# Normalising the next image on two engines: the even channel chunks of every image move from ScalarE to VectorE

## The chip, the cores and the metric

The kernel runs on one core of a Trainium2 chip. A core has a matrix engine (TensorE, PE in the profile; its weight loads are shown as PEld), a vector engine (VectorE, DVE), an activation engine (ScalarE, ACT), a general engine (GpSimd, POOL) and a synchronising engine (SyncE, SP). Each engine executes its own list of instructions strictly in that list's order, and semaphores order the lists against each other. POOL, SP and ACT also issue transfers (DMAs). The metric is the device time of one execution in microseconds (us), as a median of several executions.

## The reference

For each of 16 images of 512 channels by 1024 positions (float32): group normalisation over 8 groups of channels, a projection to query, key and value, attention in 4 heads of 128 channels, an output projection, and the image itself added at the end.

```python
xg = x.reshape(b, 8, -1)
xn = ((xg - mean(xg)) * rsqrt(var(xg) + 1e-5)).reshape(b, c, h, w)
xn = xn * norm_gamma + norm_beta
qkv = einsum('oc,bchw->bohw', qkv_w, xn) + qkv_b
q, k, v = split(qkv, 3)                       # 4 heads of 128 each
attn = softmax(q @ k.T * 128 ** -0.5)         # 1024 x 1024 per head
out = attn @ v
out = einsum('oc,bchw->bohw', proj_w, out) + proj_b
return x + out
```

## The kernel before

The kernel walks through 512 steps: 16 images, 4 heads each, 8 blocks of 128 keys per head. A step computes the scores of one block against all 1024 queries (two matmuls of 512 columns, L764), their exponential on ScalarE (L770), and, one step later, the weighted sum with the values (L860). VectorE adds the exponentials up (`tot`, L776 and L778). Between these, `plan_head` puts the other work of neighbouring images into the steps of a head:

- in head 1 of image b: the output projection of image b-1 (`proj_groups`, tiles `pp_...`), the loading of image b+1, its statistics, and then its normalisation (`normalise`, in steps 5 and 6, two channel chunks of 128 in each, each chunk in two halves of 512 columns);
- in head 2: queries and keys of the first two heads of image b+1 (`qk_groups`); in head 3: its values (`v_groups`).

The projections are done by Strassen's scheme at two levels. At the outer level, sums of the blocks of x are formed (`sums_of_b`, L280: `x` in place, then `xt`). At the inner level there are four groups of products. In a group, `make_sum` (L533) builds sums t1 to t4 on VectorE, and PE multiplies seven products in the order p1, p2, p6, p5, p7, p4, p3 (`strassen`). p1 and p2 take unsummed blocks, p6 takes t2, p5 takes t1, p7 t3, p4 t4. Products land in two accumulators `x` and `y`; ScalarE copies some out (L458, L581), and VectorE combines them into `r` (L583). The accumulator tag `y` has two buffers, so p5 of a group cannot begin before VectorE has combined p2 of the same group.

The output projection ends in `finish` of `proj_groups`: VectorE writes a tile `y` (L743), POOL issues a transfer that adds the image to it in place (L747, `accum_op`), waits until that has landed, and issues the transfer to `out` (L748). The tiles come from `ypool`, tag "y", with four buffers; eight such tiles are written per image, so the writing of a later one waits until the transfer to `out` of the tile four before it has landed.

Statistics are reduced on ScalarE (L243 to L249), combined by `stats_group` on PE, VectorE and POOL (L50 to L78), and give a scale `sc` and a shift `sh` per channel. `Norm.apply` then works in place on a half chunk, either as an activation on ScalarE (L85) or as a two-operation instruction on VectorE (L88). In image 0, whose normalisation stands before everything else, odd chunks go to ScalarE and even ones to VectorE; for every later image all chunks go to ScalarE.

The program is not issued in source order: a planner simulates the work with its own cost estimates and lays out one list of instructions for each engine. `tc.high_priority` moves the copies out of the accumulators, the combinations and the exponentials forward. So a change in one operation's engine can move others in every list.

Of the kernel before, what the change touches and what calls it, by code (L numbers as in the profile page):

```python
# [162 lines left out]
def fast_path(ctx, tc, x, sources, out, consts, flag, dims):  # L163
# [68 lines left out]
    norm = Norm(nc, gn, ps_a, avg, neghalf, gamma_sb, beta_sb, NCC, N, "y")  # L232
# [22 lines left out]
    def normalise(b, c, half):  # L255
        t = xs[b, c][:, ts(half, HALF)]
        sc, sh = scaled[b]

        return norm.apply(t, t, sc, sh, c, b > 0 or c % 2 == 1)


    def halves(tiles, prefix):
# [494 lines left out]
    def where(s):  # L757
        bh, j = divmod(s, NB)
        return (*divmod(bh, HEADS), j)
# [242 lines left out]
    def plan_head(b, h):  # L1002
# [9 lines left out]
        elif h == 1:  # L1012
            if b > 0:
                spread(plan, staggered(proj_groups(b - 1)), 0, NB)
            if b + 1 == B:
                plan[0].append(lambda: last_loads("x"))
            else:
                plan[0].append(lambda: load_x(b + 1))
                spread(plan, [lambda c=c: stats_chunk(b + 1, c) for c in range(NCC)], 2, 4)
                plan[4].append(lambda: stats_group(b + 1))  # L1020
                for r in range(2):
                    plan[5 + r] += [
                        lambda c=c, half=half: normalise(b + 1, c, half)
                        for c in range(KC * r, KC * r + KC) for half in range(NH2)
                    ]
                plan[6].append(lambda: x_sums(b + 1, (1,)))
# [41 lines left out]
    for half in range(NH2):  # L1068
        for c in range(NCC):
            ins = normalise(0, c, half)  # L1070
            last_normal = ins if c % 2 == 0 else last_normal
# [15 lines left out]
    for s in range(steps + 1):  # L1087
        units = []
        if s < steps:
            b, h, j = where(s)  # L1090
# [159 lines left out]
```

## Time and profile before

| | |
|---|---|
| median of 3 runs | 3227.11 us (3226.0 to 3231.77) |
| the profiled execution | 3226.0 us, of which its span 3224.1 us |
| PE busy | 3161.0 us (98% of the span) |
| VectorE busy | 2563.3 us (80%) |
| ScalarE busy | 1440.8 us (45%) |
| GpSimd busy | 565.7 us (18%) |
| normalisation on ScalarE (L85) | 124 instructions, 814 ns each |
| normalisation on VectorE (L88, image 0 only) | 4 instructions, 542 ns each |
| mean granted TensorE clock | 0.999 |

A line of a timeline gives the start, the time from the start of the first to the end of the last instruction of the row, the engine, the source line, the operation, output and inputs by the program's names, the shapes and the number of instructions; in square brackets the idle time of the engine just before and what ended it. Instructions on one engine overlap a little, so that two starts can be closer together than the duration of one. A table by windows gives, for each stretch of time, its length, the busy time of the five engines with the number of instructions, the granted TensorE clock, the busy share of the DMA engines and what they moved.

### The profile page before, as it was taken

The page shows a single profiled execution, that of the slowest core. Times are in us where ns is not written, and L with a number is a line of the kernel's source. Part 1 is how long each engine was busy: PE and PEld are TensorE (multiplying, and loading weights), DVE is VectorE, ACT ScalarE, POOL GpSimd, SP SyncE. Part 2 cuts the span into 40 slices and gives each one's busy share as a digit, 9 for nine tenths or more (in the row PEclk, how much of TensorE's full clock was granted, in tenths as well). Part 3 has the DMA queues.
Part 4 walks back from the last instruction along what each step waited for, and adds up shares of the span by engine and source line. Part 5 has one row for each costly group of instructions (what it writes and reads, how often), then busy time and mean ns, then how long its engine had stood idle before and what let it go on. Part 6 is the DMA issues. An engine that isn't in the chain of part 4 may idle for free.

```text
span 3224.1 us, 33936 instructions
## 1 busy us (share of the span) xinstructions
PE 3161.0 (98%) x10474; PEld 2185.4 (68%) x10474; DVE 2563.3 (80%) x4505; ACT 1440.8 (45%) x2709; POOL 565.7 (18%) x922
## 2 busy tenths in 40 slices
PE   8999999999999999999999999999999999999999
PEld 6566676676667766676666666667666676666764
DVE  8878878787887878777787777987878877788774
ACT  2535435354353543534435454453534445344332
POOL 0011212112121121211212111121111211112110
PEclk9999999999999999999999999999999999999999
DMA  5654655546555465554655546465464654646541
GB/s 168 220 180 131 201 157 153 180 131 206 157 171 166 129 198 160 175 165 128 201 159 168 168 125 205 156 179 165 125 195 154 186 177 124 188 147 193 166 128 49
DMA packets 217067, 526.92 MB, mean 163 GB/s; under 512 B 32816, under 2 KB 65840, under 8 KB 216880
## 3 DMA queue, kind: packets, MB, share of 16 engines
q1 hardware_dynamic: 128992, 276.88, 28.0%
q0 software_dynamic: 73920, 212.39, 22.2%
q10 hardware_dynamic: 13968, 35.41, 3.4%
q8 instruction: 86, 1.41, 0.2%
q14 instruction: 101, 0.83, 0.1%
HBM read 389.56 MB, written 135.00 MB: 163 GB/s over the span
## 4 chain that ended last, share of the span: by engine, by line
PE 66%; issue 19%; DVE 6%; DMA 6%; POOL 2%; ACT 0%; SPq 0%; POOLq 0%; ACTq 0%; DVEq 0%
PE s L764 18%; PE po L860 18%; PE qk_x L563 10%; PE qk_y L563 7%; PE v_x L563 6%; PE v_y L563 4%; DMA y<-in_x 3%; DVE qk_t L533 2%; DMA out_y<-y 2%; DVE xt L280 1%; DVE qk_r L583 1%; POOL y L747 1%; DVE part L789 1%; POOL rstd L67 0%; DVE tt L787 0%
## 5 line engine op out<-in xcount | busy, mean ns | idle before, releaser
L764 PE MATMUL s<-qk,qk 128*128 128x512 f32 x2048 | 1048.2, 593 | 3.2 <-ACT p L770 3.2
L860 PE MATMUL po<-p,v 128*128 128x512 f32 x2048 | 1049.4, 594 | 0.0
L770 ACT ACTIVATE p<-s 128x512 f32<-128x512 f32 x1024 | 610.4, 597 | 943.5 <-PE s L764 934.5
L860 PEld LDWEIGHTS po<-p,v 128*128 128x128 f32 x2048 | 605.0, 302 | 326.8 <-issue 219.6
L778 DVE TENSOR_TENSOR tot<-tot,p 128x1024 f32<-128x1024 f32 x385 | 469.8, 1220 | 175.4 <-ACT p L770 173.7
L764 PEld LDWEIGHTS s<-qk,qk 128*128 128x128 f32 x2048 | 387.7, 190 | 96.9 <-issue 31.4
L563 PEld LDWEIGHTS qk_x<-qk_t,w 128*128 128x128 f32 x1344 | 251.7, 190 | 168.1 <-issue 76.3
L563 PE MATMUL qk_x<-qk_t,w 128*128 128x256 f32 x1344 | 356.4, 382 | 1.4 <-ACT qk_u L458 1.4
L458 ACT COPY qk_u<-qk_x 128x512 f32<-128x512 f32 (+1 forms) x256 | 136.3, 533 | 231.6 <-PE qk_x L563 226.2
L720 POOL DMA_DIRECT2D vd<-vu x120 | 66.9, 559 | 918.7 <-DVE vu L712 916.7
L747 POOL DMA_DIRECT2D y<-in_x x120 | 109.4, 1038 | 537.2 <-DVE y L743 525.0
L563 PE MATMUL pp_x<-pp_t,w_proj 128*128 128x256 f32 x630 | 169.3, 385 | 20.8 <-ACT pp_p L458 20.8
L583 DVE TENSOR_TENSOR qk_r<-qk_y,qk_u 128x512 f32<-128x512 f32 (+1 forms) x256 | 157.4, 615 | 36.9 <-ACT qk_u L458 22.8
L563 PEld LDWEIGHTS pp_x<-pp_t,w_proj 128*128 128x128 f32 x630 | 116.0, 190 | 90.1 <-ACT pp_p L458 29.6
L725 POOL DMA_DIRECT2D v<-vd x240 | 140.7, 593 | 190.6 <-DMA vd<-vu 87.2
L563 PE MATMUL v_x<-v_t,w_v 128*128 128x256 f32 x630 | 166.6, 381 | 0.0
L583 DVE TENSOR_TENSOR v_r<-v_y,v_u 128x512 f32<-128x512 f32 (+1 forms) x120 | 76.3, 636 | 110.6 <-ACT v_u L458 80.3
L537 POOL DMA_DIRECT2D kept_t<-qk_t x240 | 143.4, 600 | 107.9 <-DVE qk_t L533 92.5
L563 PEld LDWEIGHTS v_x<-v_t,w_v 128*128 128x128 f32 x630 | 118.4, 190 | 55.3 <-issue 19.1
L563 PE MATMUL qk_y<-x,w 128*128 128x256 f32 x512 | 141.7, 379 | 0.0
L655 DVE SCALAR_TENSOR_TENSOR qk<-qk_r,qkb_sb,qk_r 128x512 f32<-128x512 f32 x192 | 137.7, 744 | 1.6
L563 PE MATMUL qk_y<-qk_t,w 128*128 128x256 f32 x448 | 119.1, 382 | 19.5 <-DVE qk_r L583 19.5
(204 smaller groups left out, 4353.5 us busy)
## 6 DMA issues: line engine op xcount, KB each, us to landing
kept_t<-qk_t POOLq DMA_DIRECT2D x180, 256.0 KB, 5.5
w<-kept SPq DMA_DIRECT2D x90, 512.0 KB, 4.3
v_t<-kept_t SPq DMA_DIRECT2D x180, 256.0 KB, 2.9
w<-kept SPq DMA_DIRECT2D x90, 384.0 KB, 3.6
rinv<-row ACTq DMA_DIRECT2D x63, 512.0 KB, 5.1
x<-in_x POOLq DMA_DIRECT2D x60, 512.0 KB, 4.9
vd<-vu POOLq DMA_DIRECT2D x120, 256.0 KB, 3.0
v<-vd POOLq DMA_DIRECT2D x240, 128.0 KB, 4.1
```

The source lines that it names most:

```text
L458: nc.scalar.copy(t[n][:, :width], t["x"][:, :width])
L537: nc.gpsimd.dma_start(t, to)
L563: nc.tensor.matmul(acc[:, ts(i, Q)], have["w"][t][:, i, slot, :], inner(i, bn), start=(first and i == 0), stop=True, skip_group_check=True,)
L583: nc.vector.tensor_add(dst, view(a), view(c))
L655: nc.vector.scalar_tensor_tensor(st[b, h][:, ts(half, HALF)], a, qkb_sb[:, i : i + 1], c, ALU.add, ALU.add)
L720: nc.gpsimd.dma_start(rows[which][ts(h, P), :], u)
L725: nc.gpsimd.dma_start(vs[b, pair][ts(q, BLK), half].rearrange("m h (k i) j -> m (h k) (i j)", k=n), rows[which].rearrange("(k m) (q e) -> ...
L747: nc.gpsimd.dma_start(t, x[b, ts(o, P), ts(half, HALF)], accum_op=ALU.add)
L764: nc.tensor.matmul(sc, ks[b, h][:, ts(j, P)], qs[b, h][:, ts(half, HALF)], start=True, stop=True)
L770: exps[s] = nc.scalar.activation(ps[s][:, ts(half, HALF)], sc, AF.Exp, scale=SCALE)
L778: added[b, h, j] = nc.vector.tensor_add(tot[b, h][:, i], tot[b, h][:, i], ps[s][:, i])
L860: nc.tensor.matmul(po[b, h][:, i], v_block(b, h, j), ps[s][:, i], start=(j == 0), stop=(j == NB - 1),)
```

## The change

In `normalise`, the condition that sends a half chunk to ScalarE loses its first alternative. For images 1 to 15, chunks 1 and 3 stay on ScalarE and chunks 0 and 2 go to VectorE, as in image 0.

```diff
     def normalise(b, c, half):
         t = xs[b, c][:, ts(half, HALF)]
         sc, sh = scaled[b]
-
-        return norm.apply(t, t, sc, sh, c, b > 0 or c % 2 == 1)
+        return norm.apply(t, t, sc, sh, c, c % 2 == 1)
```

`Norm.apply` (L81 to L88) is as before:

```python
        if on_scalar:
            return self.nc.scalar.activation(
                xn, x, AF.Identity, bias=sh[:, i], scale=sc[:, i]
            )
        return self.nc.vector.tensor_scalar(xn, x, sc[:, i], sh[:, i], ALU.mult, ALU.add)
```

The lines after it have numbers lower by one in the changed kernel.

## The prediction

> **What bounds the kernel now.** I read the page's busy table first, then the table by windows of 40 us, then PE's own timeline for its gaps, and last, around one image's gaps, the timelines of VectorE, POOL and ScalarE. PE is the bound:
>
> ```profile
> PE 3161.0 (98%) x10474; PEld 2185.4 (68%) x10474; DVE 2563.3 (80%) x4505; ACT 1440.8 (45%) x2709; POOL 565.7 (18%) x922
> ```
>
> Work that moves off ScalarE (45%) is worth nothing by itself. What counts is where PE is idle, and in windows that is one place per image, the end of head 1, where the moved instructions are. Around the normalisation of image 8:
>
> ```profile
> 1480.00:1520.00 40.00, 40.00 (x135) 28.21 (x134) 31.07 (x62) 25.43 (x58) 1.41 (x3) 1.00 0.34 106
> 1520.00:1560.00 40.00, 36.99 (x123) 25.12 (x122) 34.26 (x71) 19.61 (x35) 16.64 (x25) 1.00 0.79 198
> 1560.00:1600.00 40.00, 39.61 (x132) 27.87 (x133) 31.16 (x50) 15.06 (x28) 4.49 (x9) 1.00 0.62 208
> ```
>
> The first busy figure is PE: 40.00, 36.99, 39.61. PE's timeline has two gaps there:
>
> ```profile
> 1532.52 0.70 PE L563 MATMUL pp_x<-pp_t,w_proj 128*128 128x256 f32 x2 [1.62 <-ACT pp_p L458]
> ...
> 1544.68 1.03 PE L563 MATMUL qk_x<-qk_t,w 128*128 128x256 f32 x4
> ...
> 1560.39 1.13 PE L563 MATMUL qk_y<-qk_t,w 128*128 128x256 f32 x4 [1.77 <-DVE qk_r L583]
> ```
>
> Gap 1 (0.95 to 1.63 us in images 2 to 15) waits for a copy on ScalarE that stands behind the first normalisation, which waits for its shift. Gap 2 (0.88 to 1.80 us in images 3 to 15, together 19.6 us) waits until VectorE has combined p2 of the second group. The middle line is p6 of the first group, which needs t2 and begins without a wait. VectorE and POOL in the same stretch:
>
> ```profile
> 1540.41 0.41 DVE L533 TENSOR_TENSOR qk_t<-x,qk_t 128x256 f32<-128x256 f32 x1
> 1544.39 1.42 DVE L743 SCALAR_TENSOR_TENSOR y<-pp_r,projb_sb,pp_r 128x512 f32<-128x512 f32 x2 [3.56 <-DMA out_y<-y]
> 1545.72 0.76 DVE L533 TENSOR_TENSOR qk_t<-qk_t,x 128x256 f32<-128x256 f32 x2
> ```
>
> ```profile
> 1532.67 2.85 POOL L747 DMA_DIRECT2D y<-in_x  x3 [3.12 <-DVE y L743]
> 1539.61 0.58 POOL L748 DMA_DIRECT2D out_y<-y  x1 [4.09 <-DMA y<-in_x]
> ```
>
> VectorE sits 3.56 us at its seventh `y` tile until the transfer of the third has left its buffer: issued at 1532.67 with the added image, sent out at 1539.61, free at 1544.39. PE survives this wait only because t1 and t2 (the last of them at 1540.41) stand ahead of it.
>
> **What the change moves.** Per image, four ScalarE instructions (814 ns, L85) become four VectorE instructions. Their price is in image 0:
>
> ```profile
> 14.97 1.92 DVE L88 TENSOR_SCALAR x<-x,sc,sh 128x512 f32<-128x512 f32 x4
> ```
>
> That is 542 ns each, and one every (1.92 - 0.54) / 3 = 0.46 us. VectorE's page total rises by 60 x 0.54 = 32 us, ScalarE's falls by 60 x 0.81 = 49 us. Neither is on the path as a sum; places decide. The changed kernel's issue lists show: PE's and SP's are the same except in image 1. ScalarE's differ only by the missing four and small swaps; a normalisation (now chunk 1) still stands just ahead of the copy of gap 1 and waits for the same shift, so **gap 1 stays**: 0. On VectorE, the same in images 2 to 15, the planner did more than insert:
>
> ```
> sh; pp_t2; L88 x_0 (both halves); y_2_1, y_3_1; pp_t3; pp_r; y_2_0, y_3_0; pp_t4;
> L88 x_2; tot; pp_r; L88 x_2; x_0, x_1 (L280); pp_r; tot;
> y_0_1, y_1_1;  t1 (2);  qk_r of p2;  t2 (2);  t3 ...
> ```
>
> Before, t1 and t2 stood ahead of `y_0_1`; now they stand behind it, and so behind its wait. No DMA moves but some stores of t1 and t2 behind two L747 on POOL; their readers come some 10 us later: 0.
>
> **The new wait, image 8.** y_2_1 is written two L88 later: 2 x 0.46 = 0.92. POOL's chain from it (6.9 us to the landing, 4.8 to leaving) shifts as a whole, so `y_0_1` starts at 1544.39 + 0.92 = 1545.3. VectorE reaches it at about 1541.3, so the transfer still ends last. `y_1_1` started 0.66 us after it, at 12.53 us after gap 1. Behind the start of `y_1_1`: itself 0.66, t1 0.67, the combination of p2 0.60, the first half of t2 0.42, hand-over 0.1 (gap 2's ended 0.06 us after VectorE): 2.45. So p6 can begin 12.53 + 0.92 + 2.45 = 15.90 us after gap 1; PE is due there at 1544.68 - 1532.52 = 12.16. **New gap 3.74 us**, in-order PE with scores and values queued behind it.
>
> All images: the start of `y_1_1` after gap 1 is 11.64 to 12.57 us in images 3 to 15 (sum 159.45), and PE is due at 12.16 wherever I looked but in image 2. Sum of new gaps 159.45 + 13 x (0.92 + 2.45 - 12.16) = 45.2 us, 2.85 to 3.78 each. In image 2 p6 is due at 13.85, `y_1_1` starts at 11.00: 0.5 us. Together **+45.7**. Lower bound if the landing does not shift (other traffic sets it): 45.7 - 14 x 0.92 = 33. Upper, if VectorE's landing wait grows by POOL's usual spread (L747 lasts 0.86 to 1.55 us): 45.7 + 14 x 0.6 = 54. I take the middle row, image 8's own chain.
>
> **Gap 2 goes.** From the start of `y_1_1` VectorE needs, by the trace's spacings, 14.6 us to the combination gap 2 waits for (which the new list puts ahead of t3 and t4 of its group, 1.3 us earlier); PE, at p6 2.45 us after that start, needs it 13.9 us later, 16.4. With 1.8 us to spare: **-19.6**; bound 0 if a step is late. What is late next is nothing that I find: t3 of that group is ready 3 us ahead of p7.
>
> **Image 1** has no projection. Here two of PE's waits (0.56 and 0.70, for exponentials behind normalisations) go, and two pairs for the values move ahead of a wait of 0.41 for weights: **-1.5**; bounds -1.9 (all four of its waits) and +1.8 (four L88 on the path).
>
> **The clock.** Image 2 shows what idle time can cost beyond itself: there a gap of 0.27 stood just before the 1.62.
>
> ```profile
> 334.00:337.50 3.50, 1.61 (x6) 0.97 (x6) 3.50 (x9) 2.02 (x4) 0.76 (x2) 1.00 0.01 2
> 337.50:341.00 3.50, 3.50 (x6) 1.37 (x5) 3.50 (x6) 2.63 (x5) 1.96 (x3) 0.51 0.75 153
> ```
>
> The granted clock fell to 0.51 for 3.5 us, 1.7 us lost, after 1.89 us idle in 3.5. Gaps of up to 1.80 alone did not cause it. New gaps of about 3.5 us are twice that, so I expect a drop in nearly all of images 3 to 15: upper 13 x 1.7 = 22, lower 0; I take 13 x 1.4 = **+18**, since part of the slow stretch may fall into the gap itself. [...]
>
> [...]
>
> **Sum.** 45.7 - 19.6 - 1.5 + 18 = +42.6 us on the profiled execution's 3226.0 us (span 3224.1 and 1.9 around it): 3268.6. The median of the runs shown is 1.1 above it, so 3269.7; I say 3269, 1.3% slower.
>
> **Rivals.**
> - New gaps without a clock drop: +25, 3251. For it: 26 gaps of 0.9 to 1.8 us kept the clock. Against: these are twice as long.
> - The landing does not shift and the clock holds: 33 - 19.6 - 1.5 = +12, 3239. For it: in image 9 the same wait ended 1.3 us earlier than in image 8, so it is not fixed.
> - Worse: gap 2 stays, or a clock drop lasts twice as long: about +20 more, 3289. For it: VectorE gets 1.83 us more work where it is 86% busy. Against: the 1.8 us to spare, and a slow PE only adds to it.
> - Faster, one mechanism: the wait for the `y` buffer vanishes (POOL's transfer leaves early). Then VectorE runs straight through, `y_1_1` starts at about 9.4 us after gap 1, p6 is not late, gap 2 goes: -21, 3206. The new gap equals gap 2's 1.5 us when `y_1_1` starts 10.3 us after gap 1, before the shift of 0.92; so the leaving transfer would have to land 2 us earlier than on average now (12.27). All 13 images speak against it.
> - That the change does nothing (within 0.2%, 6.5 us, about what a measurement can tell) needs the landing some 1.5 us earlier and a clock that holds: 45.7 - 14 x 1.5 - 21.1 = +4.
>
> **How the numbers follow.** Forecast 0.54, no clock drop 0.22, no shift 0.08, worse 0.07, faster 0.06, no change 0.03. Slower holds the first four, 0.91. The range leaves out faster, no change, and half of the worst: from 3239 to 3292.
>
> **What would show it.** After: a gap of about 3.5 us at `qk_x<-qk_t` (p6) some 12 us behind gap 1 in images 3 to 15, ended by VectorE; VectorE's list with L743 waiting for `out_y` about as long as now and `qk_t` behind it; no gap 2; slices with the clock at 0.5 behind the new gap; gap 1 as before. Wrong if L743 no longer waits, if gap 1 goes too (20.7 us in images 2 to 15), or if the clock holds.

## The result, and the profile after

The changed kernel takes 3269.89 us (median of 5, 3263.51 to 3271.43) against 3229.22 us (median of 5) for the kernel before: ratio 1.0121, 95% interval 1.0106 to 1.0136. It is 1.2% slower; 3269 us was forecast. The profiled execution took 3269.89 us, span 3268.1 us, mean granted TensorE clock 0.992. The page's busy row:

```profile
PE 3183.4 (97%) x10474; PEld 2197.0 (67%) x10474; DVE 2590.0 (79%) x4565; ACT 1404.8 (43%) x2649; POOL 564.4 (17%) x922
```

The span grew by 44.0 us. PE's busy time accounts for 22.4 of it (3161.0 to 3183.4, for the same 10474 matmuls, so these ran slower), and PE's idle time for 21.6 (63.1 to 84.7). The view of PE's waits (us in total, times, longest) says where it is idle; first the kernel before:

```profile
PE pp_x L563 <- ACT pp_p L458: 20.8, 14, 1.6
PE qk_y L563 <- DVE qk_r L583: 19.5, 13, 1.8
```

and the changed kernel:

```profile
PE qk_x L562 <- DVE qk_t L532: 39.9, 14, 3.4
PE pp_x L562 <- ACT pp_p L457: 21.9, 14, 1.6
```

Gap 1 (`pp_x`) stayed, gap 2 (`qk_y`) went, and a wait of p6 (`qk_x`) for VectorE's sums came: 39.9 - 19.5 + 1.1 = 21.5 us, which is all the new idle time. Image 8 on PE's timeline of the changed kernel:

```profile
1550.76 0.70 PE L562 MATMUL pp_x<-pp_t,w_proj 128*128 128x256 f32 x2 [1.62 <-ACT pp_p L457]
...
1566.07 2.04 PE L562 MATMUL qk_x<-qk_t,w 128*128 128x256 f32 x4 [2.99 <-DVE qk_t L532]
...
1581.59 1.03 PE L562 MATMUL qk_y<-qk_t,w 128*128 128x256 f32 x4
```

p6 in the second row waits 2.99 us and then takes 2.04 instead of 1.03 us: the clock is at half. The third row is p5 of the second group, where gap 2 was. VectorE's timeline at the same place shows what p6 waits for:

```profile
1562.78 1.54 DVE L742 SCALAR_TENSOR_TENSOR y<-pp_r,projb_sb,pp_r 128x512 f32<-128x512 f32 x2 [3.22 <-DMA out_y<-y]
1564.23 0.75 DVE L532 TENSOR_TENSOR qk_t<-x 128x256 f32<-128x256 f32 x2
1564.90 0.68 DVE L582 TENSOR_TENSOR qk_r<-qk_y,qk_p 128x512 f32<-128x512 f32 x1
1565.51 0.75 DVE L532 TENSOR_TENSOR qk_t<-x,qk_t 128x256 f32<-128x256 f32 x2
```

t1 (second row) and t2 (last row) stand behind the tile that waits for its buffer, and p6 starts when the first half of t2 is there. POOL's side of that buffer:

```profile
1551.82 2.84 POOL L746 DMA_DIRECT2D y<-in_x  x3 [4.03 <-DVE y L742]
1557.90 0.58 POOL L747 DMA_DIRECT2D out_y<-y  x1 [3.24 <-DMA y<-in_x]
```

From issue to leaving is 6.08 us here; the kernel before had 6.94. The clock, by windows placed behind three gaps of the changed kernel (length, then busy times; the granted clock is the third figure from the end):

```profile
758.00:761.50 3.50, 3.34 (x12) 2.62 (x13) 3.50 (x9) 1.07 (x2) 3.08 (x5) 1.00 0.66 149
...
1146.00:1149.50 3.50, 3.38 (x5) 1.79 (x6) 3.50 (x8) 2.92 (x6) 2.19 (x3) 0.53 0.35 67
...
1566.00:1569.50 3.50, 3.43 (x8) 2.84 (x9) 3.50 (x8) 0.59 (x1) 3.22 (x5) 0.51 0.65 141
```

Behind the new gap of image 8 (last row) it is 0.51 for 3.5 us. Behind that of image 4 (first row, gap 3.06 us) it holds, and behind gap 1 of image 6 (middle row, 1.62 us) it drops. Images 2 to 14 have 12 half-clock stretches, nine of 3.41 us and three of twice that; about 1.7 us are lost in each 3.41: 25.6 us of clock, part of it inside gaps. The kernel before had one such stretch there.

### The profile page after: what moved, and what is told of

Read it like the earlier page. It is cut to its first block, busy times and chain, and to the rows that moved or that the text cites. A ratio compares the mean times of both kernels' runs of the same rounds, so it can differ in the third digit from the quotient of the medians.

```text
span 3268.1 us, 33904 instructions
## 1 busy us (share of the span) xinstructions
PE 3183.4 (97%) x10474; PEld 2197.0 (67%) x10474; DVE 2590.0 (79%) x4565; ACT 1404.8 (43%) x2649; POOL 564.4 (17%) x922
## 4 chain that ended last, share of the span: by engine, by line
PE 71%; issue 20%; DMA 5%; POOL 2%; DVE 2%; ACT 0%; POOLq 0%; SPq 0%; DVEq 0%; ACTq 0%
PE s L763 19%; PE po L859 19%; PE qk_x L562 12%; PE qk_y L562 8%; PE v_x L562 6%; PE v_y L562 4%; DMA y<-in_x 2%; DMA out_y<-y 2%; POOL y L746 1%; DVE y L742 1%; POOL rstd L67 0%; PE v_x L672 0%; PE lx L943 0%; POOL out_y L747 0%; DVE qk_t L532 0%
## 5 line engine op out<-in xcount | busy, mean ns | idle before, releaser
L777 DVE TENSOR_TENSOR tot<-tot,p 128x1024 f32<-128x1024 f32 x385 | 469.7, 1220 | 176.4 <-ACT p L769 173.9
L562 PE MATMUL qk_x<-qk_t,w 128*128 128x256 f32 x1344 | 365.7, 389 | 41.0 <-DVE qk_t L532 39.9
L582 DVE TENSOR_TENSOR qk_r<-qk_y,qk_u 128x512 f32<-128x512 f32 (+1 forms) x256 | 158.3, 618 | 51.2 <-ACT qk_u L457 37.8
L582 DVE TENSOR_TENSOR v_r<-v_y,v_u 128x512 f32<-128x512 f32 (+1 forms) x120 | 76.1, 634 | 110.5 <-ACT v_u L457 80.3
L711 DVE STREAM_TRANSPOSE vu<-vt 128x512 f32<-128x512 f32 x120 | 134.7, 1122 | 1.4 <-DMA vd<-vu 1.4
```

The source lines that it names most:

```text
L562: nc.tensor.matmul(acc[:, ts(i, Q)], have["w"][t][:, i, slot, :], inner(i, bn), start=(first and i == 0), stop=True, skip_group_check=True,)
L582: nc.vector.tensor_add(dst, view(a), view(c))
L711: nc.vector.transpose(u.rearrange("p (q i j) -> p j q i", q=n, i=BLK), t.rearrange("p (j q i) -> p j q i", q=n, i=BLK),)
L777: added[b, h, j] = nc.vector.tensor_add(tot[b, h][:, i], tot[b, h][:, i], ps[s][:, i])
```

## The experiments

The theory: VectorE's work does not matter by its amount, but by what stands behind the wait for the output buffer. The rivals: the four added VectorE instructions are a cost by themselves; or it is the clock. Each ratio is to the kernel before, run beside it on the same chip; its median there was 3232.74 us (E1 to E4), 3222.72 (E5, E6), 3220.71 (E7 to E9) and 3223.69 (E10, E11).

**E1 and E2: take away what the tile waits for.** In the changed kernel (E1) and in the kernel before (E2), the last two output tiles of an image are written into a half of an accumulator that is no longer read, instead of into `ypool`.

```diff
...
-        R = {}
+        R = r_tiles[name] = {}
...
-            t = ypool.tile([P, HALF], F32, tag="y", name=f"y_{b}_{o}_{half}")
+            if which == "c12":
+                t = r_tiles[f"pp_{b}"][2][:, 1, r, :]
+            else:
+                t = ypool.tile([P, HALF], F32, tag="y", name=f"y_{b}_{o}_{half}")
```

> The changed kernel, with the last two output tiles of an image (y_0_1, y_1_1) written into a used-up half of R[2] in place of the ypool, so that VectorE needn't wait for a buffer there. Theory (t1 and t2 stand behind that wait): no wait at the seventh tile, the new gap of 1.2 to 3.4 us at p6 goes, gap 2 stays away, the clock holds behind p6: 3203 to 3212 us, below the kernel before. Rival A (four more instructions on a VectorE 86% busy there cost what they last, wherever they stand): still slower than before, 3240 to 3265 us.

> The kernel before with the same other buffer for the two tiles. Theory: the 3.4 us wait on VectorE goes, and with it gap 2 (19.6 us in all): 3204 to 3212 us, the same as the run with the changed kernel to within 5 us, since then the engine of the normalisation decides nothing. Rival A: 25 to 45 us below the changed kernel with the same buffers. If gap 2 has another cause: 3226 us.

E1 took 3206.76 us, ratio 0.992 (0.9904 to 0.9937); E2 3201.48 us, ratio 0.9906 (0.989 to 0.9923), 2.5 us below its range. PE's waits and VectorE at image 8 in E1:

```profile
PE pp_x L562 <- ACT pp_p L457: 22.1, 14, 1.6
```

```profile
1534.01 1.41 DVE L745 SCALAR_TENSOR_TENSOR pp_r<-pp_r,projb_sb,pp_r 128x512 f32<-128x512 f32 x2
1535.34 0.76 DVE L532 TENSOR_TENSOR qk_t<-x 128x256 f32<-128x256 f32 x2
1536.01 0.68 DVE L582 TENSOR_TENSOR qk_r<-qk_y,qk_p 128x512 f32<-128x512 f32 x1
1536.61 0.75 DVE L532 TENSOR_TENSOR qk_t<-x,qk_t 128x256 f32<-128x256 f32 x2
```

In E2 gap 1 is likewise the one wait of head 1 that is left:

```profile
PE pp_x L563 <- ACT pp_p L458: 21.3, 14, 1.6
```

The order on VectorE in E1 is that of the changed kernel, but the tile no longer waits, and of the two gaps of head 1 only gap 1 is left. PE's busy time fell to 3160.0 us; besides the end one half-clock stretch is left. So the wait for the buffer is the cause of the new gap and with it of the slow clock, and in the kernel before it is the cause of gap 2 as well, since E2 has no gap 2 either. Without that wait the two divisions of the normalisation differ by 5.3 us, 0.16%, a little more than the 5 us that were expected; the runs of the two do not overlap (3203.65 to 3208.05 us against 3200.57 to 3202.94), and the cause of this rest stays open.

**E3 and E4: order alone.** E3 is the changed kernel with t1 and t2 of the first group put ahead of the tile again. E4 is the kernel before, normalisation all on ScalarE, with t1 held behind the eighth tile.

```diff
+            early = sums == "keep" and g == 0 and m in ("t1", "t2")
+            with tc.high_priority(URGENT) if early else ExitStack():
...
```

```diff
...
+            late_sums = sums == "keep" and g == 0 and m == "t1" and (b - 2) in final_y
+            with tc.issue_after(final_y[b - 2].ins) if late_sums else ExitStack():
...
-            nc.vector.scalar_tensor_tensor(
+            final_y[b] = nc.vector.scalar_tensor_tensor(
```

> The changed kernel, with t1 and t2 of the first group of queries and keys given the priority of the copies, so that VectorE does them ahead of the seventh output tile again; wait, buffers and the four moved instructions stay. Theory: the new gap at p6 goes, the clock holds, gap 2 comes back at 1.5 to 2.5 us: 3222 to 3240 us. Rival A: 3255 to 3272 us.

> The kernel before (normalisation all on ScalarE), with t1 of the first group held behind the eighth output tile: the order of the changed kernel without its change of engine. Theory: a gap at p6 of some 2.0 us (12.27 + 0.66 + 0.67 + 0.52 - 12.16), gap 2 goes, the clock drops in about half of the images: 3232 to 3256 us. Rival A: order alone costs nothing, 3222 to 3231 us.

E3 took 3226.95 us, ratio 0.9982 (0.9973 to 0.9992); E4 3243.59 us, ratio 1.0045 (1.003 to 1.0061). The waits of E3, then of E4:

```profile
PE pp_x L566 <- ACT pp_p L457: 22.3, 14, 1.6
PE qk_y L566 <- DVE qk_r L586: 13.1, 13, 1.1
```

```profile
PE qk_x L568 <- DVE qk_t L536: 24.6, 23, 2.3
```

With the sums ahead of the tile the changed kernel has the gaps of the kernel before (gap 2 back, 1.07 us in most images) and, within 0.2%, its time; with the sums behind it the kernel before gets the new gap without one instruction more on VectorE, and the clock dropped in eight of its images, in two of them behind gap 1. So the order costs. The four added instructions led the planner to that order; the loss is larger with them (1.2% against 0.45%). In image 8 the last tile then starts 12.80 us after gap 1 (12.44 in E4), and p6 another 2.51 us later (1.90 in E4, whose list has half of t2 ahead of a combination).

**E5: half of the change.** Only chunk 2 goes to VectorE.

```diff
-        return norm.apply(t, t, sc, sh, c, c % 2 == 1)
+        return norm.apply(t, t, sc, sh, c, (b > 0 and c == 0) or c % 2 == 1)
```

> Half of the change: only chunk 2 goes to VectorE, chunk 0 stays on ScalarE (two instructions per image moved, not four). In its list the first half of t1 stands ahead of the seventh output tile, the second half and t2 behind it. Theory: the third tile isn't delayed, p6 is late by 12.27 + 0.66 + 0.34 + 0.52 - 12.16 = 1.6 us per image, too short for the clock, and gap 2 goes: 3220 to 3236 us, no half of the loss. Rival A (work): half of it, 3240 to 3252 us.

3222.05 us, ratio 0.9998 (0.9988 to 1.0007).

```profile
PE qk_x L562 <- DVE qk_t L532: 17.9, 12, 2.4
```

Half the change is not half the loss. The new gap is 17.9 us in all and replaces gap 2 at about its price, and the clock fell twice at this place (images 4 and 11, gaps of 2.28 and 2.42 us). In image 8 the planner put half of t1 ahead of the waiting tile, so PE waits for less behind it.

**E6: the clock by itself.** The changed kernel with ten idle matmuls of 128 columns ahead of p6 in images 2 to 15, so that PE is not idle for as long.

```diff
+    fill = {f"qk_{b}_0_0": 10 for b in range(2, B)}
...
+            if name in fill:
+                t["y"] = bank("y")
+                for _ in range(fill[name]):
+                    nc.tensor.matmul(t["y"][:, :P], avg, ones_sq, start=True, stop=True, ...)
             mm(t["x"], 6, False)
...
```

> The changed kernel, with ten idle matmuls of 128 columns (about 2.1 us) ahead of p6 of the first group in images 2 to 15, into the accumulator that p5 overwrites: work that nobody needs, inside the new gap. Theory (the clock's drop behind the gap is a cost of its own, some 22 us in all): the granted clock holds behind p6 and the time falls to 3242 to 3256 us although PE has more to do. Rival B (the gap alone costs, the clock's drop is hidden): 3266 to 3274 us, or more.

3250.62 us, ratio 1.0085 (1.0068 to 1.0102), span 3251.6. The idle matmuls by line, and the waits:

```profile
L474 PE MATMUL qk_y<-ones_sq,avg 128*128 128x128 f32 x280 | 33.5, 275 | 0.0
```

```profile
PE pp_x L571 <- ACT pp_p L458: 14.3, 14, 1.6
PE qk_x L571 <- DVE qk_t L541: 14.0, 14, 2.1
...
PE qk_y L571 <- DVE qk_r L591: 6.3, 13, 0.5
```

The clock dropped once. PE's busy time is 3194.6 us; without the 33.5 of the idle matmuls 3161.1, the 3161.0 of the kernel before. So the 22.4 us of extra busy time in the changed kernel are the clock. The span fell by less, 16.5 us: the idle matmuls and the rest of the wait are together 47.5 us in place of 39.9, gap 1 is 7.6 less, and 6.3 us of gap 2 came back. That last wait belongs to this run's own list, in which sums for later products stand ahead of the combination it waits for: this starts 13.8 us after p6 in image 8, against 11.4 us in image 4 of the changed kernel, where the clock held as well.

**E7, E8 and E9: can gap 1 go too?** All normalisations of an image are put into step 6, and those on ScalarE are held behind the copy that PE waits for in gap 1. E7: kernel before, other buffer (as in E2) and this; E8: changed kernel, other buffer and this; E9: kernel before and this alone.

```diff
-        return norm.apply(t, t, sc, sh, c, b > 0 or c % 2 == 1)
+        on_scalar = b > 0 or c % 2 == 1
+        after = copies.get((f"pp_{b - 2}_3", "p1")) if on_scalar else None
+        with tc.issue_after(after.ins) if after is not None else ExitStack():
+            return norm.apply(t, t, sc, sh, c, on_scalar)
...
-                    plan[5 + r] += [
+                    plan[6] += [
```

> The kernel before, with the last two output tiles of an image in the used-up half of R[2], and every normalisation of images 2 to 15 on ScalarE held behind the copy that PE waits for in gap 1 (the copy of p1 of the output projection's last group). Theory: gap 1 is there only because that copy stands behind an activation that waits for the shift. The second edit then takes away nearly all of gap 1 (20 to 22 us in all) on top of gap 2 (19.5 us): 37 to 45 us below the kernel before on the same chip, ratio 0.986 to 0.9885, and no PE wait for pp_p above 0.5 us. Rival: what PE waits for there is the combination chain of the projection's last groups, or the later normalisation makes the first sums for queries and keys late: then no better than the other buffer alone (ratio about 0.9906), with the idle time at pp_x or at qk_y and qk_x.

> The changed kernel with the same two edits (tiles in the used-up half of R[2]; the normalisations that are left on ScalarE held behind the copy of p1). Theory that the division between VectorE and ScalarE by itself is worth next to nothing once no buffer is waited for: within 5 us of the kernel before with the same two edits, ratio 0.986 to 0.990. Rival (four more instructions on VectorE per image are on the path by themselves, or a shorter normalisation is a gain by itself): over 8 us apart in either direction.

> The kernel before with the normalisations on ScalarE held behind the copy of p1 alone; output tiles in their four buffers as before. Theory: gap 1 goes (20 to 22 us), gap 2 stays, since the wait for the buffer that the transfer to the output leaves is as before: ratio 0.992 to 0.995, the wait of qk_y for qk_r 15 to 30 us in all. Rival: PE reaching the end of head 1 earlier only meets the same landing, so gap 2 grows by what gap 1 loses: ratio 0.998 to 1.001 and 35 to 40 us of waiting there.

E7 3195.17 us, ratio 0.9921 (0.9904 to 0.9937); E8 3195.72 us, 0.992 (0.9903 to 0.9937); E9 3239.12 us, 1.0058 (1.0041 to 1.0075). The ratios of all three miss what the theory gave; E8's distance from E7 does not. The waits of E7, then of E9:

```profile
PE pp_y L568 <- DVE pp_r L588: 13.8, 17, 1.6
```

```profile
PE qk_x L568 <- DVE qk_t L538: 28.9, 14, 3.9
```

The copy was the releaser of gap 1, since no wait for `pp_p` is left. But in most images 0.76 us turn up some 7 us later at `pp_y`, where PE now arrives before VectorE's combination of the products. The theory for E7 named the wait rightly and overlooked the next one. In E9 neither forecast came: the price is at p6, as in the changed kernel, with all normalisation on ScalarE. VectorE at image 8 in E9:

```profile
1550.65 0.75 DVE L748 SCALAR_TENSOR_TENSOR y<-pp_r,projb_sb,pp_r 128x512 f32<-128x512 f32 x1 [2.62 <-issue]
1552.22 0.75 DVE L748 SCALAR_TENSOR_TENSOR y<-pp_r,projb_sb,pp_r 128x512 f32<-128x512 f32 x1 [0.81 <-DMA out_y<-y]
1552.89 0.42 DVE L538 TENSOR_TENSOR qk_t<-x,qk_t 128x256 f32<-128x256 f32 x1
```

Again the planner laid the waiting tiles ahead of half of t2. E7 is E9 with the other buffer, and 44 us faster. E8 and E7 are 0.55 us apart (E8's PE waits 8.5 us at `pp_y` and 4.3 us for ScalarE ahead of p6, E7's 13.8 us at `pp_y`): with both edits, where the normalisation runs is worth nothing that can be measured. With the other buffer alone it was 5.3 us (E1 and E2).

**E10 and E11: what the second edit adds.** E2's and E7's kernels on one chip.

> The kernel before with the last two output tiles in the used-up half of R[2] and nothing else, run again so that it stands on one chip beside the version that also holds the normalisations behind the copy of p1. Theory (waits of PE add up): gap 1 of 21 us is here and a wait of 14 us for pp_r there, so this one is 5 to 9 us slower than the other. Rival (chips differ, and the second edit brings nothing or costs, as the ratios 0.9906 and 0.9921 from two chips suggest): equal within 2 us, or this one the faster.

> The kernel before with both edits, on the same chip. Theory: 5 to 9 us below the other buffer alone, its PE waiting some 14 us for pp_r at pp_y and not for pp_p. Rival: equal within 2 us or slower, ratio to the kernel before 0.991 to 0.993.

E10 3201.56 us, ratio 0.9929 (0.9916 to 0.9943); E11 3195.2 us, ratio 0.9911 (0.9898 to 0.9925). Gap 1 in E10 is 16.9 us (less than E2's 21.3), the wait at `pp_y` in E11 13.2. By the medians the second edit brings 6.4 us more. The runs of the two overlap (3196.05 to 3204.78 against 3191.45 to 3199.41 us), so the rival is unlikely rather than excluded. Of the 6.5 us between the profiled spans 2.2 are busy time of PE: E10 had three half-clock stretches there, E11 none. The kernel before with both edits is the fastest version found: 28.5 us below the kernel before on this chip.

## Why the prediction was right

- **The bound and the cause.** "t1 and t2 stood ahead of `y_0_1`; now they stand behind it, and so behind its wait": shown by E1 (wait gone, gap gone), E3 and E4 (order alone gives and takes the gap). The page totals moved by +26.7 us on VectorE and -36.0 on ScalarE, not by +32 and -49: neighbouring instructions overlap (in the kernel before, the busy times of ScalarE's groups add up to 1515.5 us, where ScalarE is busy for 1440.8), so a mean duration times a number of instructions puts the busy time too high. Nothing else rested on these two.
- **The new gaps, +45.7, measured +39.9.** Images 3 to 15 have 36.8 us (1.16 to 3.36 each) in place of 45.2. The mis-sized term is the shift of the landing, 2 x 0.46 = 0.92 us: in the ten of these images where the clock held behind gap 1, `y_1_1` starts on average 0.57 us later after gap 1 than in the kernel before, which makes 3.5 us less. In image 8 `y_0_1` starts 1562.78 - 1550.76 = 12.02 us after gap 1, against 1544.39 - 1532.52 = 11.87 before, only 0.15 later: POOL's transfers landed sooner (6.08 us from issue to leaving, not 6.94), so the chain did not shift as a whole. In images 6, 9 and 10 the clock was at half behind gap 1, which the prediction did not have: PE was due there 14.01 us after gap 1, 1.69 later, which makes 5.1 us less in gaps (they count as clock), and their tiles came later too (+1.5 us). The remaining step is one of counting: the view counts a wait from the end of the matmul before, 12.32 us after gap 1, while the prediction counted from 12.16, where p6 began in the kernel before, overlapping that matmul (2.1 us less). From the start of `y_1_1` to p6 it took 2.50 us, 2.45 forecast (+0.7).
- **Image 2, 0.5 us, measured 3.11.** p6 was put as due 13.85 us after gap 1 there. That spacing held the half-clock stretch of 1.7 us that the kernel before has behind this gap. In the changed kernel the clock held after image 2's gap 1, and p6 was due 15.43 - 3.11 = 12.32 us after it, as in image 8. So the prediction took clock time for a fixed distance.
- **Gap 2, -19.6, measured -19.5.** "1.8 us to spare": in image 4, at full clock, the combination ends at 770.25 and p5 begins, unhindered, at 772.00.
- **Gap 1, 0, measured +1.1.** As forecast; E7 shows its releaser was the one named.
- **Image 1, -1.5.** PE's waits there are 0.51 and 1.33 us, against 0.56, 0.70, 0.41 and 0.25 before: about even. A small miss.
- **The clock, +18, measured +22.4** of busy time; E6 shows that it is the clock. "A drop in nearly all of images 3 to 15" was not how it went: in images 4, 12 and 15 it held after gaps of 3.06, 2.87 and 3.17 us, while three stretches lasted twice as long and three followed gap 1. The misses offset each other, so that the size is near is in part luck: the length of the gap was the wrong measure (last section).
- **The sum, +42.6, measured +44.0 in the span (+40.7 by the medians of five runs each).** Too much for the gaps (5.8), too little for the clock (4.4), for gap 1 (1.1) and for image 1: the total is nearer than its terms, and that is luck.
- **The rivals.** No clock drop: falls, by E6. Landing that does not shift: partly true (0.57 of the 0.92 us came in the ten images above), but with the clock falling none the less. Faster, with the wait for the buffer gone: did not happen by itself; E1 made it happen, and took 3206.76 us where this rival gave 3206, though the kernel before took 3232.74 us beside E1 and 3229.22 beside the changed kernel.

Image 2's row, from which the clock term was worked out (half clock behind gaps of 0.27 and 1.62 us), gave about the right size, not the right images. The L88 row held: in the changed kernel its 64 instructions have a median of 541 ns, and 542 were read in image 0. A float32 TENSOR_TENSOR takes 418 ns for 128x256 there (L532), 685 for 128x512 (L582) and 1220 for 128x1024 (L622), by which some 150 ns do not grow with the size (an estimate from these three). L88 is faster than a TENSOR_TENSOR of its size; why, the runs do not show.

## What to carry to other kernels

When an edit adds instructions to an engine that executes in order, look first at which of its instructions wait for a buffer or a transfer, and then at what the new list puts behind them: here such an order cost 1.2% with four more instructions per image and 0.45% with none. A tile that waits for a slow round trip (transfer in with addition, transfer out: in image 8 of the changed kernel 6.08 us from the issue of the first to the issue of the second) is best given a buffer that is free in any case; that took away both the loss and gap 2 (E1 and E2). A price read as the spacing of two events in one image should be checked for slow-clock stretches inside it before it is used. And what an idle gap costs in clock should not be priced by its length alone: in the changed kernel no slow stretch followed gaps of 3.06, 2.87 and 3.17 us, and one followed each of three gaps of 1.62 and 1.63 us.

## What the runs showed of the hardware that was not expected

The length of a gap alone does not decide whether the clock is halved. In the changed kernel gaps of 1.60 to 1.63 us were followed by it in images 6, 9 and 10 and not in ten others; gaps of 2.79 to 3.36 us were followed by it in nine images, for twice the time in three of them, and gaps of 3.06, 2.87 and 3.17 us were not. In E10 three gaps of 1.62 us (images 6, 9 and 14) had it.

Most of these cases go with where the gap lies. In the changed kernel the half-clock stretches start at 350.89, 555.69, 958.47, 1146.20, 1361.24, 1566.04 us and so on, whole multiples of 3.413 us apart to within 0.01 us. So its trace can be cut into pieces of 3.413 us with a border at the start of every stretch, and a gap that crosses a border is shared by two pieces. Image 4 and image 8, each the piece ahead of the one in which the clock held or fell:

```profile
753.69:757.10 3.41, 1.41 (x4) 0.57 (x2) 2.11 (x5) 1.19 (x2) 0.00 (x0) 1.00 0.86 214
1562.63:1566.04 3.41, 0.45 (x2) 0.00 (x1) 3.23 (x7) 0.81 (x2) 0.36 (x1) 1.00 0.62 151
```

The 3.06 us of image 4 are cut into 1.99 and 1.08 us, and the clock held; of the 2.99 us of image 8, 2.96 lie in one piece, and it fell. Images 12 and 15 were cut likewise (1.87 and 1.00, 2.00 and 1.17), while gap 1 of images 6, 9 and 10 lay whole in one piece, which with the small pauses around it was idle for 1.74, 1.81 and 1.73 us. In images 2 to 15 of the changed kernel the clock fell after each of the nine full-speed pieces with 2.19 to 3.14 us of idle time, after these three of the 17 with 1.60 to 2.00 us, and after none with less. A second slow piece followed in the three images in which PE was idle for 0.66, 0.74 and 1.16 us in the first, and in none of the nine with 0.46 us or less. In images 2 to 15 of the kernel before, cut in the same way from its one stretch, the clock fell after the one piece with 1.83 us and after none of the others, which have 1.64 us at most. That the clock goes by the idle time of such pieces is the author's estimate from these counts; no run was made to test it, and what decides between 1.60 and 2.00 us stayed open. Counted from the start of the span, the pieces begin at 2.73 us in the changed kernel and at 3.01 us in the kernel before, so which images are hit is probably not to be read from the program (an estimate too).

A later issue need not land later by as much: POOL's chain from adding the image to leaving was 0.86 us shorter in image 8 when VectorE wrote the tile later, though each of its steps is the same instruction. Over the whole execution the median from issue to landing went from 6.5 to 5.7 us for the transfer that adds the image, and from 3.9 to 4.4 us for the one to `out`. The runs do not show why. And the kernel before had medians from 3220.71 to 3232.74 us in the groups of runs, 0.37% apart and more than some of the differences measured here. The record gives the same chip number, 3, for both of these extremes (E7 to E9, and E1 to E4), so this spread is not shown to be one between chips, as the expectation of E10 had it. Either way, ratios from different groups could not rank E2 and E7; E10 and E11, run beside each other, set them 6.4 us apart.
